# A gated graph network and three SAGE passes in one kernel: loads of the gated weights, the seam of first and second SAGE pass, and tiles cleared earlier

## The chip, the cores and the metric

The kernel runs on one core of one Trainium2 chip. A core has five engines that run their own instruction streams and wait for each other by semaphores: TensorE (PE, with its weight loads shown apart as PEld), VectorE (DVE), ScalarE (ACT), GpSimd (POOL) and SyncE (SP, which only issues DMAs here). ACT and POOL issue DMAs too. All DMAs run on the same 16 DMA engines. The metric is device time in microseconds, lower is better.

## What is computed

The input is a batch of 16 graphs with 1024 nodes and 128 features, and a dense adjacency of zeros and ones. Two layers follow each other, each with a residual and a layer norm:

```python
x = _layernorm(x + gnn0(x, adj, nodemask, ...))
x = _layernorm(x + gnn1(x, adj, nodemask, ...))

# gnn0: 4 gated layers
h = x
for i in range(4):
    hw = einsum('bnc,cd->bnd', h, weight[i])
    m = einsum('bjn,bjd->bnd', adj, hw)
    h = gru_cell(m, h, w_ih[i], w_hh[i], b_ih[i], b_hh[i])

# gnn1: a pattern of removed neighbours, and 3 SAGE passes on what is left
adj_d = adj * keep(adj > 0, mask)          # sequential over the rows
h1 = bn(relu(sage(x, adj_d, Wr1, Wx1, b1)))
h2 = bn(relu(sage(h1, adj_d, Wr2, Wx2, b2)))
h3 = bn(relu(sage(h2, adj_d, Wr3, Wx3, b3)))
out = concat([h1, h2, h3]) @ Wl + bl
# sage: ((adj_d @ x) / deg) @ Wr + x @ Wx + b, each row divided by its length
# bn: statistics over all graphs and nodes, so a pass ends before the next begins
```

The kernel is built on properties of the adjacency (zeros and ones, a pattern that settles at once). It tests them while it runs and has a general version for inputs where they don't hold. The tests are the "look" operations named below.

## The kernel before

**Stages.** A gated stage (class `Gated`, with the removal pattern, class `FixPoint`, woven into it), then the first, second and third SAGE pass (class `Sage`), and a last stage with the layer norm. Inside the gated stage and inside each pass the order of every engine's instructions is the one written in the code; each engine works through its list and waits in order. What stands between two passes (`Sage.run`, `weights`) is ordered by the tile scheduler.

**Lead-in of the gated stage.** `Gated.run` (from L1130) loads x of the first graph on POOL, calls `load_weights`, takes the first step of the removal pattern (four loads `f_a` on POOL), and loads the eight adjacency blocks `h_a` of the first graph on POOL. `load_weights` (L947) issues, for each of four layers, the weight (64 KB, `h_w`), `w_ih` and `w_hh` (192 KB each, in rows of 512 bytes), and then two small biases, all from ACT's queue. `prepare` transposes them on PE, multiplies the weight into `w_ih`, and copies the results by DVE (`w_ih`, `h_wi`) and ACT (`w_hh`, `h_wh`). Then PE begins the first layer's aggregation (L1092). ACT splits x into a rounded part and a rest (`begin_rows`, L1056) before its copies; POOL makes the rest (L1057) and only then loads the second graph.

**Gated layers.** Two graphs run in turn. A layer aggregates on PE (L1092), then computes the gates by products L1104, with sigmoids and tanh on ACT (L1113, L1119, L1122), two operations on DVE (L1116, L1118) and the state update on POOL (L1123 to L1125). All products use six PSUM banks `h_g`, in turn. While one graph's gates are computed, the other's state is transposed (L1037), rounded on ACT (L1025), and its rest is made on DVE (L1030). Steps of the removal pattern stand between these on DVE and ACT (L864, L866, L777, L737). Once a layer of the first graph ends, `load_test` loads one test block into `h_test` (a single buffer) on SP, and `check` tests it on DVE (L2028) within the second graph's next layer.

**First pass.** `slot(b, t)` writes 16 slots for each graph b, preparing graph b+1 in the same slots. It holds four buffers `p_a` for test blocks; `load_a` loads one on SP (L1491) and `check` tests it on DVE (L2028). For graph b the blocks 2 and 3 are loaded in slots 10 and 13 of the graph before, blocks 4 to 7 in slots 0, 2, 5 and 8, and the tests of blocks 2 to 7 are in slots 2, 5, 8, 10, 12 and 14. The chain of a graph: aggregation of x (slots 0, 1, 3, 4), copies to `s_ag` (slots 2 and 5, `evict`, L1601, two buffers in turn, shared with the copies of slot 15 that SP stores in slot 1 of the next graph, L1733), degrees, products `p_oa` and `p_ob` (slots 5 and 7), scaling on DVE (`scale_rows`, L1395 and L1396, slots 6 and 8), squares on ACT, rows (slots 7 and 9), their split (slots 8 and 10), the turn of the rows on PE with copy and statistics (`turn_r`, L1450, L1631, L1632, slots 11 and 13), and the second aggregation, of the rows (slots 9, 10, 12 and 14). SP stores the turned rows in slots 13 and 15 (L1717).

The order on SP within a slot is: `load_a` at its beginning, and the stores at its end.

**Seam.** After the last slot `Sage.run` computes the batch norm from the statistics and scales three weight matrices by it (`weights`, L1328 to L1366), with a small product `s_v` in a PSUM pool that takes over the first pass's banks, splits the result into three parts on DVE (L1343 to L1350), creates buffers, and clears the three `s_rho` tiles on POOL (L2014). Then `second` issues its loads (`load_second`, `load_bytes`) and its first products L1800, L1803, L1806.

Of the kernel before, what the change touches and what calls it, by code (L numbers as in the profile page):

```python
# [8 lines left out]
F32 = mybir.dt.float32  # L9
BF = mybir.dt.bfloat16  # L10
# [11 lines left out]
P = 128  # L22
B = 16
N = 1024
C = 128
NB = N // P
HF = 512
# [890 lines left out]
class Gated:  # L918
# [28 lines left out]
    def load_weights(self):  # L947

        nc, wk = self.nc, self.wk
        weight, w_ih, w_hh, b_ih, b_hh = self.given  # L950
        self.w = wk.tile([P, 4, P], F32, name="h_w")
        self.w_in = {}
        names = iter(n for n in "h_ms h_r h_z h_zh".split() for _ in range(2))
        for l in range(L0):
            nc.scalar.dma_start(self.w[:, l, :], weight[l])
            for n, src in enumerate((w_ih, w_hh)):
                t = wk.tile([C, HF], F32, name=next(names))
                t = self.w_in[l, n] = t[:, :3 * C].rearrange("p (g c) -> p g c", g=3)
                nc.scalar.dma_start(t, src[l].rearrange("(g p) c -> p g c", p=C))
        t = wk.tile([P, NB, C], F32, name="h_x", bufs=3)  # L960
        self.b_in = [t[:L0 * 3, i, :] for i in range(2)]
        for t, src in zip(self.b_in, (b_ih, b_hh)):
            nc.scalar.dma_start(t, src.rearrange("l (g c) -> (l g) c", c=C))

    def prepare(self):
        nc, ident = self.nc, self.cst["ident"]
# [24 lines left out]
    def load_test(self, n):  # L991
        if n < B * 2:
            self.test = self.wk.tile([P, N], F32, name="h_test", bufs=1)
            self.nc.sync.dma_start(self.test, self.adj[n // 2, n % 2 * P:(n % 2 + 1) * P, :])

    def check(self, n):
        junk = self.wk.tile([P, N], BF, name="h_junk", bufs=1)
# [212 lines left out]
class Sage:  # L1210
# [61 lines left out]
    def constants(self):  # L1272

        nc, ident, K = self.nc, self.cst["ident"], 3 * B
        const = self.const
        self.one16 = const([P, 1], 0.0, "s_one16", F16)
        nc.vector.memset(self.one16[:1, :], 1.0)
        nc.gpsimd.memset(self.row, 0.0)

        self.sel01 = const([10, 3, 6], 0.0, "s_sel01")  # L1280
        for i in range(3):
            nc.vector.tensor_copy(self.sel01[:, i, 3:], ident[:10, 3 * i:3 * i + 1].to_broadcast([10, 3]))
        self.ones = const([P, P], 0.0, "s_ones", BF)
        nc.vector.memset(self.ones[:6, :], 1.0)
        nc.gpsimd.memset(self.r6, 0.0)
        nc.gpsimd.memset(self.graph, 0.0)
        nc.vector.tensor_add(self.part6, ident[:6, 0:3], ident[:6, 3:6])
        self.part48 = const([K, 3], 1.0, "s_part48")
        for base, m in ((0, 1), (B - 1, -1)):
            nc.gpsimd.affine_select(self.part48, self.part48, pattern=[[-m * B, 3]], compare_op=ALU.is_ge,  # L1290
                                    fill=0.0, base=base, channel_multiplier=m)
        nc.vector.tensor_add(self.graph[:K, :], ident[:K, :B], ident[:K, B:2 * B])
        nc.vector.tensor_add(self.graph[:K, :], self.graph[:K, :], ident[:K, 2 * B:K])

        mask, junk = self.cst["mask"], self.wxp[:, 0, :].rearrange("p (a b) -> p a b", a=NB)
        nc.vector.scalar_tensor_tensor(junk, mask, 0.0, mask, op0=ALU.is_gt, op1=ALU.not_equal,
                                       accum_out=self.bad[:, BAD - 1:BAD])

        drop = self.wr2
        nc.vector.tensor_copy(drop, ident)  # L1300
        nc.vector.memset(drop[:1, :], -1.0)
        nc.vector.memset(drop[:1, :1], 0.0)
        nc.gpsimd.memset(self.mask48, 0.0)
        nc.vector.memset(self.mask48[:B, :], 1.0)
# [33 lines left out]
    def parts(self, v, part, out):  # L1338

        nc, shape = self.nc, list(v.shape)  # L1340
        rest = self.small.tile(shape, F32, name="s_rest")
        p = [self.small.tile(shape, BF, name=f"s_part{i}") for i in range(3)]
        nc.vector.tensor_copy(p[0], v)  # L1343
        nc.vector.tensor_sub(rest, v, p[0])
        nc.vector.tensor_copy(p[1], rest)
        nc.vector.tensor_sub(rest, rest, p[1])
        nc.vector.tensor_copy(p[2], rest)
        nc.vector.tensor_scalar(out, p[0], part[:, 0:1], None, op0=ALU.mult)
        for i in (1, 2):
            nc.vector.scalar_tensor_tensor(out, p[i], part[:, i:i + 1], out, op0=ALU.mult, op1=ALU.add)  # L1350

    def weights(self, l, v):

# [100 lines left out]
    def first(self):  # L1454

        nc, tc, cst = self.nc, self.tc, self.cst
        with ExitStack() as c:
            pool = lambda name, **k: c.enter_context(tc.tile_pool(name=name, **k))

            self.atp = [pool("p_at0", bufs=1)]  # L1460
            self.sp = pool("p_s", bufs=2)
            xp = pool("p_x", bufs=1)
            self.wk = pool("p_wk", bufs=2)
            self.atp.append(pool("p_at1", bufs=1))
            self.nrp = [pool(f"p_nr{i}", bufs=1) for i in range(2)]
            self.ap = pool("p_a", bufs=4)
            self.ps1 = pool("p_ps1", bufs=1, space=PSUM)
            self.ps2 = pool("p_ps2", bufs=2, space=PSUM)

            self.ps3 = pool("p_ps3", bufs=3, space=PSUM)  # L1470
            c.enter_context(tc.manual_schedule(engines={ET.PE, ET.DVE, ET.Activation, ET.Pool, ET.SP}))
            self.g = {}
            self.load_nr(0, 0)
            self.load_nr(0, 1)
            self.load_s(0)
            self.eps = self.const([P, 1], 1e-5, "s_eps")

            self.xh = xp.tile([P, NB, C], FR, name="p_xh")
            self.xl = xp.tile([P, NB, C], FR, name="p_xl")
            for t, v in ((self.xh, 1.0), (self.xl, 0.0)):  # L1480
                nc.vector.memset(t[:, :, :1].bitcast(F32), v)
            self.row = xp.tile([P, N], F16, name="p_row")
            self.constants()
            for b in range(-1, B):
                for t in range(16):
                    self.slot(b, t)
# [147 lines left out]
    def slot(self, b, t):  # L1634

        nc, g, n = self.nc, self.g.get(b), b + 1
        now, nxt = b >= 0, n < B

        if nxt:
# [3 lines left out]
                self.load_s(n + 1)  # L1643
            if t in (10, 13):
                self.load_a(n, 2 + t // 13)
        if now and t in (0, 2, 5, 8):
            self.load_a(b, (0, 2, 5, 8).index(t) + 4)

        if now:
            if t in (2, 5):  # L1650
# [11 lines left out]
        if now:  # L1662
# [3 lines left out]
            if t in (0, 1, 3, 4):  # L1666
                f, lo = t // 3, t in (1, 4)
# [5 lines left out]
            if t in (6, 8):  # L1673
                f = t // 8
# [6 lines left out]
            if t in (7, 9):  # L1681
                f = t // 9
# [2 lines left out]
                self.split_r(b, t // 10)  # L1685
            if t in (6, 8):
                g["ss", t // 8] = self.squares(g["o", t // 8])
            if t in (11, 13):
                self.turn_r(0, b, t // 13, self.ps1)
            if t in (9, 10, 12, 14):  # L1690
                part = g["rl"] if t in (10, 14) else g["rh"]
                js = range(4 * (t // 12), 4 * (t // 12) + 4)
# [5 lines left out]
        if nxt:  # L1698
# [5 lines left out]
                self.turn_x(n, t // 8)  # L1704
            if t in (7, 12):
                self.split_x(n, t // 12)
        if now and t in (2, 5, 8, 10, 12, 14):
            self.check(b, (2, 5, 8, 10, 12, 14).index(t) + 2)

        if now:  # L1710
            if t == 2:
                nc.sync.dma_start(self.at8[b, 1], g["b", 1])
            if t == 7:
                for i in range(3):
                    nc.sync.dma_start(self.rho[b, i:i + 1, :], g["rho"])
            if t in (13, 15):
                nc.sync.dma_start(self.rt[b, t // 15], g["rt", t // 15])  # L1717
        if nxt:
            if t == 10:
                nc.sync.dma_start(self.at8[n, 0], self.g[n]["b", 0])  # L1720
# [282 lines left out]
    def run(self):  # L2003
        tc, nc = self.tc, self.nc
        self.first()
        with tc.tile_pool(name="s_psw", bufs=1, space=PSUM) as ps:
            self.weights(1, ps.tile([6, C], F32, name="s_v6"))
        accp = self.ctx.enter_context(tc.tile_pool(name="s_acc", bufs=1))
        self.acc = accp.tile([P, B, NB, C], F32, name="s_acc")
        self.rt_kept = accp.tile([C, HF], F32, name="s_rtl")  # L2010
        self.ahead = self.ctx.enter_context(tc.tile_pool(name="s_ahead", bufs=1))
        self.rhos, self.layers = [self.ahead.tile([P, N], BF, name=f"s_rho{i}") for i in range(3)], 0
        for t in self.rhos:
            nc.gpsimd.memset(t, 0.0)  # L2014
        self.second()
        with tc.tile_pool(name="s_psw", bufs=1, space=PSUM) as ps:
            self.weights(2, ps.tile([6, C], F32, name="s_v6"))
        self.r3 = self.ctx.enter_context(tc.tile_pool(name="s_r3p", bufs=1)).tile([C, B, 2, HF], F32, name="s_r3")
        self.third()
        with tc.tile_pool(name="s_psw", bufs=1, space=PSUM) as ps:  # L2020
            r48 = self.head_weights(ps)
        self.last(r48)
# [94 lines left out]
```

## Time and profile before

| | us |
|---|---|
| median of 3 runs (2174.55 to 2177.75) | 2175.93 |
| the profiled execution | 2176.16 |
| its span, first to last instruction | 2174.3 |
| gated stage's first aggregation on PE begins at | 33.81 |
| first pass's last turn of rows copied at | 1742.93 |
| second pass's first product L1800 begins at | 1751.40 |

Times within the profile are microseconds from the start of the span. In a line of the timeline the columns are: start, duration, engine, line, operation, output<-inputs, shapes and count; in brackets stands how long the engine was idle before it and what it waited for. A line of the table of windows gives for a stretch: its length, then busy time and number of instructions of PE, PEld, DVE, ACT and POOL, the TensorE clock granted (1.00 is full), the busy share of the DMA engines, and GB/s.

### The profile page before, as it was taken

What the parts mean: (1) busy time and instruction counts of PE and PEld (TensorE: products, weight loads), DVE (VectorE), ACT (ScalarE), POOL (GpSimd) and SP (SyncE); (2) the same over time, 40 slices, a digit from 0 to 9 for tenths busy, and PEclk for the clock granted to TensorE, in tenths of its full rate; (3) what the DMA queues carried; (4) which work ended last, traced back from release to release, by engine and by line L of the source; (5) the groups of instructions that cost most, each with busy time, mean ns of one, the idle gap of its engine ahead of it and who ended that gap; (6) DMA issues with size and microseconds to landing.
All of it is one profiled execution on the core that took longest, in us unless ns stands there. A gap on an engine that the chain in (4) does not pass through costs nothing. (4 is left out here: it accounts for less than half of the span.)

```text
span 2174.3 us, 33161 instructions
## 1 busy us (share of the span) xinstructions
PE 2063.3 (95%) x10217; PEld 1438.1 (66%) x10217; DVE 1831.1 (84%) x4313; ACT 1312.8 (60%) x3142; POOL 1324.3 (61%) x1346
## 2 busy tenths in 40 slices
PE   6999999999999999999999978999999889999987
PEld 3666556666556665566655656777777768887876
DVE  4898998988998889998889978888888777676888
ACT  3657557566565656656566466666666545555757
POOL 4458558567467476476575456777777545555852
PEclk9999999999999999999999989999999999999989
DMA  8348356347446276455394349888888677775515
GB/s 258 77 93 252 92 126 225 82 133 214 101 143 195 75 210 155 96 190 132 79 266 104 74 166 318 305 297 307 304 305 306 209 243 271 265 262 185 158 40 157
DMA packets 233856, 406.16 MB, mean 187 GB/s; under 512 B 79042, under 2 KB 100196, under 8 KB 233668
## 3 DMA queue, kind: packets, MB, share of 16 engines
q1 hardware_dynamic: 187844, 284.37, 40.7%
q0 software_dynamic: 41472, 117.46, 20.1%
q10 hardware_dynamic: 4352, 2.11, 0.4%
q8 instruction: 83, 1.36, 0.3%
q14 instruction: 105, 0.86, 0.1%
HBM read 313.48 MB, written 109.25 MB: 194 GB/s over the span
## 5 line engine op out<-in xcount | busy, mean ns | idle before, releaser
L1104 PE MATMUL h_g<-h_h,h_wh 128*128 128x512 f32 x768 | 396.1, 597 | 3.3 <-DVE h_r L1116 3.3
L1104 PE MATMUL h_g<-h_ms,h_wi 128*128 128x512 f32 x768 | 392.3, 592 | 0.0
L1123 POOL TENSOR_TENSOR h_zh<-h_r,h_h 128x512 f32<-128x512 f32 x126 | 174.1, 1382 | 257.9 <-ACT h_r L1119 254.7
L737 DVE TENSOR_TENSOR_SCAN f_rank<-f_a,f_first,f_pd 128x1024 f16<-128x1024 bf16 x128 | 299.4, 2345 | 4.2
L1092 PE MATMUL h_g<-h_a,h_hi 128*128 128x512 f32 x1024 | 278.6, 413 | 1.1 <-DMA h_a<-in_adj_dram 1.0
L1536 POOL CAST p_b<-p_at 128x512 uint8<-128x512 f32 x256 | 219.4, 878 | 84.3 <-DVE p_at L1528 52.3
L1104 PEld LDWEIGHTS h_g<-h_ms,h_wi 128*128 128x128 f32 x768 | 145.6, 190 | 184.2 <-issue 168.6
L1092 PE MATMUL h_g<-h_a,h_lo 128*128 128x512 f32 x1024 | 261.9, 393 | 0.4 <-DVE h_lo L1030 0.4
L1092 PEld LDWEIGHTS h_g<-h_a,h_hi 128*128 128x128 f32 x1024 | 190.1, 188 | 61.7 <-issue 21.0
L1092 PEld LDWEIGHTS h_g<-h_a,h_lo 128*128 128x128 f32 x1024 | 189.8, 188 | 39.0 <-DVE h_lo L1030 0.8
L1104 PEld LDWEIGHTS h_g<-h_h,h_wh 128*128 128x128 f32 x768 | 133.4, 190 | 100.3 <-issue 72.9
L1125 POOL TENSOR_TENSOR h_h<-h_h,h_zh 128x512 f32<-128x512 f32 x126 | 179.9, 1427 | 9.9
L1119 ACT ACTIVATE h_r<-h_r,h_bi 128x512 f32<-128x512 f32 x128 | 92.4, 722 | 150.1 <-DVE h_r L1118 150.1
L1124 POOL TENSOR_TENSOR h_zh<-h_z,h_zh 128x512 f32<-128x512 f32 x126 | 162.0, 1285 | 9.9
L1095 ACT COPY h_ms<-h_g 128x512 f32<-128x512 f32 x128 | 73.8, 576 | 150.7 <-PE h_g L1092 150.7
L1403 ACT ACTIVATE s_junk<-s_o 128x128 bf16<-128x128 f32 x256 | 76.1, 298 | 141.6 <-DVE s_o L1396 141.6
L910 ACT ACTIVATE f_u<-f_rank,f_q 128x128 f16<-128x128 f16 (+7 forms) x128 | 110.6, 867 | 69.7 <-DVE f_rank L850 69.7
L2028 DVE SCALAR_TENSOR_TENSOR p_junk<-p_a 128x1024 bf16<-128x1024 f32 x96 | 125.8, 1311 | 0.0
L1803 PE MATMUL q_ob<-s_wxp,q_xt 128*128 128x256 f32 x512 | 123.5, 385 | 0.0
L778 POOL TENSOR_SCALAR_AFFINE_SELECT f_both<-f_both 128x512 bf16<-128x512 bf16 x32 | 20.4, 639 | 164.2 <-DVE f_both L777 164.2
L1528 DVE SCALAR_TENSOR_TENSOR p_at<-p_nr,p_u 128x128 fp32r<-128x128 bf16 (+1 forms) x192 | 102.4, 543 | 20.2 <-ACT p_at L1520 14.8
L887 ACT ACTIVATE f_pd<-f_rank,f_q 128x128 f32<-128x128 f16 x128 | 59.1, 462 | 96.6 <-DVE f_q L701 93.4
(273 smaller groups left out, 4900.9 us busy)
## 6 DMA issues: line engine op xcount, KB each, us to landing
h_a<-in_adj_dram POOLq DMA_DIRECT2D x128, 512.0 KB, 9.1
p_a<-in_adj_dram SPq DMA_DIRECT2D x96, 512.0 KB
f_a<-in_adj_dram POOLq DMA_DIRECT2D x128, 256.0 KB, 6.5
e_nr<-f_nr SPq DMA_DIRECT2D x128, 256.0 KB
p_nr<-e_nr SPq DMA_DIRECT2D x32, 1024.0 KB
h_test<-in_adj_dram SPq DMA_DIRECT2D x32, 512.0 KB
s_at<-p_b SPq DMA_DIRECT2D x32, 512.0 KB
s_ag<-s_ag SPq DMA_DIRECT2D x64, 256.0 KB
```

The costliest lines, as they stand in the source:

```text
L737: nc.vector.tensor_tensor_scan(out, a, other[:, 0, 0:1].to_broadcast([P, N]), start, op0=ALU.add, op1=ALU.bypass)
L910: nc.scalar.activation(u[:, :n1], rank[:, g, :n1], AF.Abs, bias=q[:, 1, g:g + 1], scale=q[:, 0, g:g + 1])
L1092: nc.tensor.matmul(pm[f], part[:, j, :], st.adj[j][:, half[f]], start=(j == 0 and n == 0), stop=(j == NB - 1 and n == 1))
L1104: nc.tensor.matmul(pg, lhs, rhs, start=(i == 0), stop=(i == len(mm) - 1))
L1119: nc.scalar.activation(r, r, AF.Tanh, bias=bias(self.bi, 2))
L1123: aid.tensor_tensor(d, r, h, ALU.subtract)
L1124: aid.tensor_tensor(d, z, d, ALU.mult)
L1125: aid.tensor_tensor(h, h, d, ALU.add)
L1528: self.nc.vector.scalar_tensor_tensor(g["at"][:, j, c0:c0 + low], v[:, j, c0:c0 + low], 0.0, pu[:, :low], op0=ALU.is_lt, op1=ALU.is_lt)
L1536: self.nc.gpsimd.tensor_copy(g["b", f][:, j, :], g["at"][:, j, f * HF:(f + 1) * HF].bitcast(F32))
L1803: nc.tensor.matmul(pb[:, i], g["xt"][:, f, blk], self.wxp, start=(i % 2 == 0), stop=False)
L2028: nc.vector.scalar_tensor_tensor(junk, a, 0.0, a, op0=ALU.is_gt, op1=ALU.not_equal, accum_out=bad[:, c:c + 1])
```

## The change

There are six edits.

1. The loads of `w_hh` and of the biases are issued by SP instead of ACT.
2. The first test block of the gated stage is loaded by POOL instead of SP; the others stay on SP.
3. The three `s_rho` tiles move into the pool that lives through all passes, and are cleared with the other constants at the beginning of the first pass, behind the clearing of `row`, instead of between the passes.
4. For the last graph of the first pass, test blocks 4 to 7 are loaded in slots 0, 0, 1 and 2 and the tests are made in slots 0 to 5; the turns of the rows are in slots 10 and 12 and their stores in slots 11 and 13.
5. The small product of the first seam gets the fourth bank of its pool, where it had the first.
6. `idle` issues products into a bank that nobody reads, four ahead of `weights(1)` and six behind it.

```diff
@@ load_weights
-                nc.scalar.dma_start(t, src[l].rearrange("(g p) c -> p g c", p=C))
+                (nc.scalar, nc.sync)[n].dma_start(t, src[l].rearrange("(g p) c -> p g c", p=C))
...
-            nc.scalar.dma_start(t, src.rearrange("l (g c) -> (l g) c", c=C))
+            nc.sync.dma_start(t, src.rearrange("l (g c) -> (l g) c", c=C))
@@ load_test
-            self.nc.sync.dma_start(self.test, self.adj[n // 2, n % 2 * P:(n % 2 + 1) * P, :])
+            (self.nc.sync if n else self.nc.gpsimd).dma_start(self.test, self.adj[n // 2, n % 2 * P:(n % 2 + 1) * P, :])
@@ constants
         nc.gpsimd.memset(self.row, 0.0)
+        for t in self.rhos:
+            nc.gpsimd.memset(t, 0.0)
@@ new function
+    def idle(self, junk, n):
+
+        for i in range(n):
+            self.nc.tensor.matmul(junk, self.cst["ident_b"], self.mask48[:, :HF], start=True, stop=True)
@@ first
             self.row = xp.tile([P, N], F16, name="p_row")
+            self.rhos, self.layers = [self.one.tile([P, N], BF, name=f"s_rho{i}") for i in range(3)], 0
@@ slot
-        if now and t in (0, 2, 5, 8):
-            self.load_a(b, (0, 2, 5, 8).index(t) + 4)
+        tail = b == B - 1
+        slots = (0, 0, 1, 2) if tail else (0, 2, 5, 8)
+        if now and t in slots:
+            for k in range(4):
+                if slots[k] == t:
+                    self.load_a(b, k + 4)
...
-            if t in (11, 13):
-                self.turn_r(0, b, t // 13, self.ps1)
+            slots = (10, 12) if tail else (11, 13)
+            if t in slots:
+                self.turn_r(0, b, slots.index(t), self.ps1)
...
-        if now and t in (2, 5, 8, 10, 12, 14):
-            self.check(b, (2, 5, 8, 10, 12, 14).index(t) + 2)
+        slots = (0, 1, 2, 3, 4, 5) if tail else (2, 5, 8, 10, 12, 14)
+        if now and t in slots:
+            self.check(b, slots.index(t) + 2)
...
-            if t in (13, 15):
-                nc.sync.dma_start(self.rt[b, t // 15], g["rt", t // 15])
+            slots = (11, 13) if tail else (13, 15)
+            if t in slots:
+                nc.sync.dma_start(self.rt[b, slots.index(t)], g["rt", slots.index(t)])
@@ run
-            self.weights(1, ps.tile([6, C], F32, name="s_v6"))
+            junk = [ps.tile([P, HF], F32, name=f"s_junk{i}") for i in range(3)][2]
+            v = ps.tile([6, C], F32, name="s_v6")
+            self.idle(junk, 4)
+            self.weights(1, v)
+            self.idle(junk, 6)
...
-        self.rhos, self.layers = [self.ahead.tile([P, N], BF, name=f"s_rho{i}") for i in range(3)], 0
-        for t in self.rhos:
-            nc.gpsimd.memset(t, 0.0)
```

## The prediction

> **What bounds the kernel now.** I read four views. The page first: TensorE (PE) is busy 95% of the span. The chain of waits holds one piece at the very end, so the chain is built from the timeline. The table of windows then shows where PE's share counts: in the gated stage (33 to 1275 us) PE is busy 297 of every 300 us, so a microsecond before that stage moves everything behind it, and so does a stall within it.
>
> ```profile
> span 2174.3 us, 33161 instructions
> PE 2063.3 (95%) x10217; PEld 1438.1 (66%) x10217; DVE 1831.1 (84%) x4313; ACT 1312.8 (60%) x3142; POOL 1324.3 (61%) x1346
> ...
> 33.00:333.00 300.00, 297.31 (x1121) 182.86 (x1122) 266.91 (x560) 180.54 (x329) 173.99 (x168) 1.00 0.50 132
> ```
>
> The timeline of 0 to 60 us shows the lead-in. See that ScalarE (ACT) is held by issuing fourteen small loads until 23.5 us, that PE waits for the weights, and that DMA is saturated (share over 1, about 385 GB/s) until 27 us.
>
> ```profile
> 18.00:21.00 3.00, 0.79 (x4) 0.39 (x2) 0.29 (x1) 0.00 (x0) 0.00 (x0) 1.00 1.13 384
> ...
> 13.23 0.90 PE L974 MATMUL h_g<-ident,h_r 128*128 128x128 f32 x3 [5.40 <-DMA h_r<-in_L_gnn_w_ih_dram]
> 17.68 0.90 PE L974 MATMUL h_g<-ident,h_r 128*128 128x128 f32 x3 [3.55 <-DMA h_r<-in_L_gnn_w_hh_dram]
> 23.50 1.28 ACT L1056 ACT_TABLE_LOAD   x1 [23.50 <-DMA h_z<-in_L_gnn_w_ih_dram]
> 23.55 0.87 PE L974 MATMUL h_g<-ident,h_z 128*128 128x128 f32 x3 [4.76 <-DMA h_z<-in_L_gnn_w_ih_dram]
> 33.81 2.09 PE L1092 MATMUL h_g<-h_a,h_hi 128*128 128x512 f32 x8
> 57.49 1.30 POOL L1125 TENSOR_TENSOR h_h<-h_h,h_zh 128x512 f32<-128x512 f32 x1
> 57.83 2.04 DVE L2028 SCALAR_TENSOR_TENSOR h_junk<-h_test 128x1024 bf16<-128x1024 f32 x1
> 67.89 0.68 DVE L1030 TENSOR_TENSOR h_lo<-h_g,h_hi 128x512 fp32r<-128x512 f32 x1
> ```
>
> The timeline of 1719 to 1757 us shows the seam. See what the first copy of the last graph waits for, who works beside the weights' product, and the clock.
>
> ```profile
> 1720.15 1.24 SPq L1733 DMA_DIRECT2D s_ag<-s_ag  x2
> 1725.10 0.59 ACT L1601 COPY s_ag<-p_ag 128x512 f32<-128x512 f32 x1 [4.06 <-DMA s_ag<-s_ag]
> 1730.76 0.67 DVE L1395 TENSOR_TENSOR s_o<-p_oa,s_rdeg 128x512 f32<-128x512 f32 x1
> 1746.05 2.87 POOL L2014 MEMSET s_rho<- 128x1024 bf16 x3 [4.12 <-DMA s_rt<-s_rt]
> 1747.14 0.83 DVE L1336 TENSOR_SCALAR s_wr<-s_wr,s_ab 128x128 f32<-128x128 f32 x1
> 1751.43 0.98 PE L1800 MATMUL q_oa<-s_wr,q_agi 128*128 128x128 f32 x3 [0.73 <-PE s_v L1366]
> 1756.12 0.69 DVE L1396 TENSOR_TENSOR s_o<-q_ob,s_o 128x512 f32<-128x512 f32 x1 [1.85 <-PE q_ob L1806]
> ...
> 1748.00:1749.00 1.00, 0.00 (x0) 0.00 (x0) 1.00 (x5) 0.00 (x0) 0.92 (x1) 0.50 1.04 397
> ```
>
> **What the Trainium skill says.** "DMA: Bandwidth & Descriptors", section on queues, rings and completion order: each DMA engine "round-robins between the queue rows it has work for", packet by packet. The trace agrees: from 17.7 to 23.5 us the ACT queue landed 256 KB (44 GB/s) of 385 GB/s, 11%, which is one 512-byte row for each 4096-byte row of the POOL queue. "SBUF — State Buffer", two separate sides: VectorE (DVE) in a two-port mode and GpSimd (POOL) lock a shared port pair for a whole instruction. The trace agrees: the 128x128 scaling at 1747.14 took 0.83 us beside POOL's memsets, the same form at 2104.13 0.28 us. "TensorE: Matmul & The Clock Gate", what's actually happening: an idle window of about 3.4 us halves the clock. Here PE stopped at 1744.75 and the window from 1748 shows 0.50, full again near 1754.7.
>
> **The change part by part**, against the profiled execution (2176.16 us, span 2174.3; the median shown is 2175.93, 0.2 less).
>
> *Gated weights' queue.* Six of ACT's fourteen loads go to SP, a third queue beside POOL's, so the weights take two turns in three instead of one in two. Before, the ACT queue moved 56 rows per DMA engine by about 6.3 us, then one per 0.184 us (56 rows from 13.2 to 23.5). After, the last weight is ACT's eighth load, row 128. I take 50 rows by 6.3; 46 at 0.22 us beside SP's 96 (0.184 plus 0.035 to 0.045 for the extra row, below the 0.055 per row seen once the adjacency tapers off): 16.4; the last 32 at 0.184: 22.3 us. ACT, with eight issues, is free long before and does the splits of x early. From the last weights' transposes (28.02) to the first aggregation (33.81) are 5.8 us of PE and copies, unchanged. New start 28.2: **-5.6 us**. Bounds: DMA now ends at 27.8; 512 KB less (the test load leaves) is 1.3 us at 400 GB/s, so the adjacency is in near 27.5 and its last block is used 1.7 us after the start: at most -8.0. If the weights only gain the room of the test load: -1.3. The second stream's loads start earlier too; they had 8 us of slack (landed by 45, used at 52.6).
>
> *First test's load on POOL.* It was on SP at 1.24 us. On POOL it stands behind the state update that ends at 58.8. Nobody waits behind it on POOL (next work 66.6), but DVE's test, at 57.8, does. A 256 KB load on a quiet POOL queue took at least 4.0 us to land; with 256 KB more at 400 GB/s, 4.6. The test then runs 63.4 to 64.6 and DVE continues 4.8 us late. Behind it: four pairs L864/L866 (1.1 each), L777 (0.5), L1116, L1118 and L1030 (0.85, 0.7, 0.7), which ends at 71.7 instead of 68.57 (before, the pairs had 1.35 of waits that vanish). The six banks go round: the product at 68.82 takes the bank that L1030 reads, so PE stalls 2.9 us, for good. Bounds: landing in 3.0 (the least of any POOL transfer of x) costs 1.3; 7.9 costs 6.2. I take **+2.9**.
>
> *Tiles cleared in lead-in.* Three memsets of 0.95 us now stand on POOL behind that of the row (1278.15). POOL was idle 1.83 of these 2.85 us; its memset of the mask ends 1.3 us later, and DVE, which had 0.16 to 0.8 us of waits there, starts its unit (1284.46) 0.5 us late: **+0.5** (0 to 1.5). POOL's next cast waited 5.8 us for a store anyway.
>
> *Last tests and loads moved.* On SP, load 6 of the last graph now stands ahead of the two stores of s_ag, and it waits for test 2, which DVE can begin at 1722.2 and end near 1723.5. The first store so leaves at 1724.0 instead of 1720.15, behind one load more on a saturated queue. Its data (by the sum of the windows' GB/s) move by 1727.1; before they were due at 23.6 and the release came 1.5 later, so the copy at 1725.10 goes to 1728.6: +3.5 (2.5 to 4.4). Below nothing it can't go: the store is only put later. On DVE four tests of 1.14 us now stand between the copy and L1395, in place of one: L1395 comes 6.3 us after the copy instead of 5.66: 1734.9, +4.1. PE idles from 1726.2 to 1729.9, 3.7 us; I take it that the clock drops as at 1748, half speed for 3.3 us, of which 0.7 reach L1395. Before, the four later tests delayed the rows by only 0.1.
>
> *Turns moved, own bank, memset gone, junk matmuls.* Measured from L1395. The last turn comes before the third part of the aggregation, so the statistics are complete 12.0 us after L1395 (14.5 before). The six scalings take about 1.3 instead of 1.9 us. PE finishes at +14.6 (14.0), and with a product near +16 doesn't go cold. The ten junk matmuls (0.22 each) fill an idle PE; if the scheduler puts them earlier, up to 1 us. What is late next is a transfer: the loads of the second pass wait for the release of the first's tiles (+14.2), and land as before 4.0 (s_ag) and 5.5 us (s_rt) after issue; so L1803 at +19.7, L1806 ends at +22.0, L1396 at +22.1 instead of 25.4: -3.3 (-2.3 to -4.3). Seam: 4.1 + 0.7 - 3.3 = **+1.5**.
>
> Sum: -5.6 + 2.9 + 0.5 + 1.5 = -0.7 us, so 2175.2.
>
> **Rivals.** (1) *The seam gives what it saves.* If the release of the s_ag buffer isn't the brake (store still in time), L1395 is 0.6 late and the seam is -2.7: sum -4.9, 2171.0. For it: PE's own result was ready at 1724.4, only 0.7 before the copy. Against: the wait of 4.06 us ended by that store. (2) *The weights come no sooner*, because DMA is saturated anyway: -1.3 instead of -5.6: +3.6, 2179.5. For: the share over 1. Against: the 11%. (3) *The test load ends on the other side*: one mechanism, DVE's in-order wait at 57.8, priced at 1 us per us of landing beyond 1.7. From a landing of 5.3 us the whole is slower than before; if it lands in 11.3, as POOL's adjacency loads did at the start, it costs 9.6 and the sum is +6.0, 2181.9. For: POOL's loads are often that long. Against: DMA moves 0 to 5 GB/s from 48 to 60 us. (4) *DVE's slack takes the test's wait*: +0.4: -3.2, 2172.7. For: DVE is busy 16.8 of 20 us there. Against: PE's slack on L1030 is 0.25 us.
>
> **How the numbers follow.** Forecast 46% (its own range 2172 to 2178), rival 1 22%, rival 2 14%, rival 3 9%, rival 4 9%. About 0.2%, 4.4 us, is what a measurement of this kernel can tell from no change. Faster by more: two thirds of rival 1, a third of 4, a twelfth of the forecast, and their mixtures: 24%. Slower by more: 0.4 of rival 2, most of 3, a twelfth of the forecast, and a rest: 19%. Within: 57%. The range 2170.0 to 2180.5 takes in the rivals' times save the upper part of 3.
>
> **What would show it.** L1092's first start near 28 us; the first L2028 waiting for h_test until 60 to 64 and a PE wait of some us near 65 (after the shift); in the seam (shifted) the copy L1601's wait for s_ag of 7 us instead of 4, L1395 some 4 us later against the last stage's begin, no POOL memset, PE clock 1.00 at the product. Wrong would make it: L1092 at 32 or later; the copy not waiting; or release of the second pass's loads ruled by something else.

## The result, and the profile after it

The changed kernel takes 2182.35 us (median of 8 runs, 2180.25 to 2184.56) against 2175.68 us before (8 runs on the same chip, 2173.92 to 2179.19): ratio 1.0030, 95% interval 1.0021 to 1.0038. It is 6.7 us slower, outside the range given. The profiled execution took 2182.17 us, its span is 2180.4 us, 6.1 more than before. From the profile page of the changed kernel (busy time of each engine, its share of the span, instructions):

```profile
PE 2063.6 (95%) x10226; PEld 1438.0 (66%) x10227; DVE 1833.3 (84%) x4313; ACT 1312.9 (60%) x3142; POOL 1325.4 (61%) x1347
```

TensorE (PE) is as busy as before to 0.3 us; what came is idle time. To find it I set the two timelines beside each other and took the start of the same product in both. In this table and below, the lead-in is the stretch from the gated stage's last transposes to the first aggregation of the first pass, and a product is called cold when it takes up to twice its usual time at a granted clock of 0.50:

| stretch, from product to product | before, us | after, us | difference |
|---|---|---|---|
| span start to first L1092 | 33.81 | 27.59 | -6.2 |
| to the first L1037 past 70 us (first test lies between) | 47.45 | 48.18 | +0.7 |
| to L1037 of the gated stage's end | 1193.19 | 1192.91 | -0.3 |
| **lead-in: to the first aggregation of the first pass** | 23.21 | 35.95 | **+12.7** |
| first pass, to the low part of its last graph | 424.74 | 422.12 | -2.6 |
| **seam: to the first L1806 (after: L1821)** | 33.30 | 37.30 | **+4.0** |
| second and third pass, to the last stage | 351.15 | 349.49 | -1.7 |
| last stage | 67.5 | 66.9 | -0.6 |

The start came near the predicted time: the last weights are turned at 20.35 instead of 28.02 us, and the first aggregation begins at 27.59. The timeline of the kernel before, then of the changed one:

```profile
28.02 1.49 PE L974 MATMUL h_g<-ident,h_zh 128*128 128x128 f32 x6
...
29.51 3.46 PE L981 MATMUL h_g<-h_wi,h_w 128*128 128x384 f32 x8
```

```profile
20.35 1.51 PE L974 MATMUL h_g<-ident,h_zh 128*128 128x128 f32 x6 [4.70 <-DMA h_zh<-in_L_gnn_w_ih_dram]
...
21.88 4.87 PE L981 MATMUL h_g<-h_wi,h_w 128*128 128x384 f32 x8
...
27.59 2.09 PE L1092 MATMUL h_g<-h_a,h_hi 128*128 128x512 f32 x8
```

Next, the first test: one line of the kernel before, then the changed kernel (L2044 there is L2028 before):

```profile
68.82 1.02 PE L1104 MATMUL h_g<-h_h,h_wh 128*128 128x512 f32 x2
```

```profile
52.52 0.59 POOL L994 DMA_DIRECT2D h_test<-in_adj_dram  x1
...
56.23 1.23 DVE L2044 SCALAR_TENSOR_TENSOR h_junk<-h_test 128x1024 bf16<-128x1024 f32 x1 [4.54 <-DMA h_test<-in_adj_dram]
...
62.41 0.74 DVE L1116 SCALAR_TENSOR_TENSOR h_r<-h_g,h_bh,h_r 128x512 f32<-128x512 f32 x1
...
63.21 1.12 PE L1104 MATMUL h_g<-h_h,h_wh 128*128 128x512 f32 x2 [0.45 <-DVE h_r L1116]
...
63.87 0.68 DVE L1030 TENSOR_TENSOR h_lo<-h_g,h_hi 128x512 fp32r<-128x512 f32 x1
```

The load is issued behind the state update and lands 3.7 us later, and DVE waits 4.54 us for it. But PE waits only 0.45 us, and its product is 0.6 us later than its old place shifted by the start (68.82 - 6.22 = 62.60).

Now the lead-in, where nearly all was lost. The timeline of the kernel before, which was not shown yet:

```profile
1274.45 0.60 PE L1037 MATMUL h_g<-ident,h_h 128*128 128x128 f32 x4
...
1278.15 0.94 POOL L1278 MEMSET p_row<- 128x1024 f16 x1 [3.35 <-ACT h_z L1122]
1278.26 0.07 DVE L1481 MEMSET p_xh<- 128x8 f32 x1
...
1282.97 0.55 POOL L1072 DMA_DIRECT2D e_sum<-h_x  x1 [0.52 <-DVE h_x L1070]
...
1284.73 0.59 PE L1515 MATMUL p_u<-ident_b,p_nr 128*128 128x128 bf16 x4 [1.72 <-DVE p_at L1528]
...
1289.29 3.95 POOL L1536 CAST p_b<-p_at 128x512 uint8<-128x512 f32 x7 [5.76 <-DMA e_sum<-h_x]
```

POOL begins p_row as soon as ACT's L1122 is done, and DVE begins p_xh without a wait; only POOL's casts (L1536) wait for the store of e_sum, 5.76 us that nobody else feels. The same stretch after:

```profile
1268.68 0.60 PE L1037 MATMUL h_g<-ident,h_h 128*128 128x128 f32 x4
...
1277.63 0.54 POOL L1072 DMA_DIRECT2D e_sum<-h_x  x1 [8.59 <-DVE h_x L1070]
...
1285.30 0.95 POOL L1278 MEMSET p_row<- 128x1024 f16 x1 [7.13 <-DMA e_sum<-h_x]
1285.37 0.07 DVE L1488 MEMSET p_xh<- 128x8 f32 x1 [8.04 <-DMA e_sum<-h_x]
...
1286.19 2.78 POOL L1280 MEMSET s_rho<- 128x1024 bf16 x3
...
1289.20 0.17 DVE L1294 TENSOR_TENSOR s_graph<-ident 48x16 f32<-48x16 f32 x1 [2.64 <-POOL s_graph L1288]
...
1292.16 0.58 PE L1523 MATMUL p_u<-ident_b,p_nr 128*128 128x128 bf16 x4 [14.48 <-DVE p_at L1536]
```

Now the memsets of p_row and p_xh themselves wait for that store. It was issued at 1277.63 and took 7.5 us to land, while the first pass's matrices were loading (DMA share 0.98 from 1275 to 1285). The same store took 6.1 us in the kernel before, and 7.7 us in run 4 below, where PE feels nothing of it: what counts is who waits for it. DVE sits idle 8.04 us. Behind it come POOL's three memsets of s_rho, for which DVE waits 2.64 us more, and PE is idle 14.48 us. That the memset of a new tile waits for a transfer of the stage before points to where the tile lies.

Last the seam: three products of the kernel before, then the timeline of the changed kernel (L1595 is now L1603, L1601 L1609, L1395 L1402, L1396 L1403):

```profile
1722.40 1.98 PE L1595 MATMUL p_ag<-p_at,p_xl 128*128 128x512 f32 x8
...
1726.51 2.11 PE L1595 MATMUL p_ag<-p_at,p_xl 128*128 128x512 f32 x8
...
1735.94 2.08 PE L1595 MATMUL p_ag<-p_at,p_rh 128*128 128x512 f32 x8 [2.12 <-ACT p_rh L1444]
```

```profile
1723.71 4.68 SPq L1499 DMA_DIRECT2D p_a<-in_adj_dram  x3
...
1726.75 1.98 PE L1603 MATMUL p_ag<-p_at,p_xl 128*128 128x512 f32 x8
...
1728.48 0.86 SPq L1748 DMA_DIRECT2D s_ag<-s_ag  x2
...
1733.89 0.58 ACT L1609 COPY s_ag<-p_ag 128x512 f32<-128x512 f32 x1 [8.49 <-DMA s_ag<-s_ag]
...
1735.31 3.76 PE L1603 MATMUL p_ag<-p_at,p_xl 128*128 128x512 f32 x8
...
1741.21 0.67 DVE L1402 TENSOR_TENSOR s_o<-p_oa,s_rdeg 128x512 f32<-128x512 f32 x1
...
1746.40 3.69 PE L1603 MATMUL p_ag<-p_at,p_rh 128*128 128x512 f32 x8 [2.13 <-ACT p_rh L1451]
...
1757.30 0.38 PE L1371 MATMUL s_v<-s_wr,s_beta 128*6 128x128 f32 x2
...
1764.53 0.69 DVE L1403 TENSOR_TENSOR s_o<-q_ob,s_o 128x512 f32<-128x512 f32 x1 [1.86 <-PE q_ob L1821]
```

And a line of the table of windows (the granted clock of PE is the third number from the end):

```profile
1733.00:1735.00 2.00, 0.00 (x0) 0.00 (x0) 0.49 (x2) 1.08 (x2) 0.00 (x0) 0.50 1.01 409
```

SP is held by three loads until 1728.4, since they wait for tests on DVE that free their buffers. The first store of s_ag so leaves 1.7 us after the low part of the last graph has begun (1728.48, against 1726.75 for that product); before it left 2.3 us ahead of it (1720.15 against 1722.40). The copy waits 8.49 instead of 4.06 us, PE stands still from 1730.5 to 1735.2, and the clock falls to 0.50. The two cold products (3.76 and 3.69 us) took 2.11 and 2.08 us in the kernel before. At the weights' product the clock is 1.00 again, and the product takes 0.38 us instead of 0.58; the turns made earlier, the own bank, the idle products and the absent memsets stand together in this trace.

### The profile page after: what moved, and what is told of

It reads as the page before. It is cut to its first block, busy times and chain, and to the rows that moved or that the text cites. A ratio compares the mean times of both kernels' runs of the same rounds, so it can differ in the third digit from the quotient of the medians.

```text
span 2180.4 us, 33182 instructions
## 1 busy us (share of the span) xinstructions
PE 2063.6 (95%) x10226; PEld 1438.0 (66%) x10227; DVE 1833.3 (84%) x4313; ACT 1312.9 (60%) x3142; POOL 1325.4 (61%) x1347
## 5 line engine op out<-in xcount | busy, mean ns | idle before, releaser
L1092 PE MATMUL h_g<-h_a,h_hi 128*128 128x512 f32 x1024 | 278.4, 413 | 0.4 <-DMA h_a<-in_adj_dram 0.4
L1092 PE MATMUL h_g<-h_a,h_lo 128*128 128x512 f32 x1024 | 262.2, 393 | 0.1
L1092 PEld LDWEIGHTS h_g<-h_a,h_hi 128*128 128x128 f32 x1024 | 190.1, 188 | 60.8 <-issue 21.0
L1092 PEld LDWEIGHTS h_g<-h_a,h_lo 128*128 128x128 f32 x1024 | 189.6, 188 | 39.3 <-DVE h_lo L1030 1.3
L2044 DVE SCALAR_TENSOR_TENSOR p_junk<-p_a 128x1024 bf16<-128x1024 f32 x96 | 125.9, 1311 | 0.1
L1523 PE MATMUL p_u<-ident_b,p_nr 128*128 128x128 bf16 x1024 | 96.8, 223 | 21.0 <-DVE p_at L1536 18.7
```

The source lines that it names most:

```text
L1092: nc.tensor.matmul(pm[f], part[:, j, :], st.adj[j][:, half[f]], start=(j == 0 and n == 0), stop=(j == NB - 1 and n == 1))
L1523: nc.tensor.matmul(pu[:, i * P:(i + 1) * P], v[:, 4 * f + i, j * P:(j + 1) * P], self.cst["ident_b"], start=True, stop=True)
L2044: nc.vector.scalar_tensor_tensor(junk, a, 0.0, a, op0=ALU.is_gt, op1=ALU.not_equal, accum_out=bad[:, c:c + 1])
```

## Experiments

Twelve kernels in three groups, each timed beside the kernel before on one chip; a ratio is to the kernel before, with its 95% interval. "Stretch" numbers are those of the table above, from each run's own profiled execution, which is one execution among several.

The place of the tiles in the on-chip memory, bytes per partition, as the programs allot it:

| pool | before | with s_rho in s_one |
|---|---|---|
| p_s | 73,440 to 81,632 | 79,584 to 87,776 |
| p_x (p_xh, p_xl, p_row) | 81,632 to 91,872 | 87,776 to 98,016 |
| h_wk of the gated stage | 96,832 to 160,320 | the same |

The three tiles, 2,048 bytes each, came out of a pool that lies below the first pass's pools and pushed all of these up by 6,144 bytes. p_x now reaches 1,184 bytes into h_wk, and h_wk also holds h_x, the source of the e_sum store. My theory: it is this reach that costs, not the memsets. Rivals: the memsets; the shift as such; an end of the gated stage that comes early and meets the same store.

**1. The start alone.** Only the edits of L959, L963 and L994.

> The kernel before with the start of the gated stage alone: the hidden weights and the biases on SP's queue, the first test's load on POOL's. The traces put this part at -6.2 us at the first aggregation and +0.7 at the test (-5.5 after it), and no other stage is touched: about 2170.3 us. If what was gained at the start were lost again at the gated stage's end whatever is done to the tiles (an earlier end meets the same store), it would be 2175.7, and PE's idle time in the lead-in of the first pass would grow to some 14 us here too.

2169.51 us, 0.9971 (0.9958 to 0.9983), as expected. The lead-in was 23.38 us, PE did not wait there. An early end of the gated stage loses nothing: that rival is out, and the start's gain reaches the end of the program.

**2. The tiles alone**, allotted in s_one and cleared in the lead-in.

> The kernel before with the three s_rho tiles taken from s_one and cleared on POOL in the lead-in of the first pass, nothing else. My theory (the place of the tiles: the pool p_x is pushed into the region of the gated stage's h_wk and all lead-in work waits for its last store): the first pass begins some 11 us later, POOL's three memsets are gone from the seam (up to -1.5 there): 2185 us, 2183 to 2188. The prediction's own price (three memsets behind one another, place without effect): +0.5, 2176.

2187.20 us, 1.0048 (1.0031 to 1.0064), with a lead-in of 36.61 us. This part alone costs 10.9 us, the whole change 6.7.

**3 and 4. Place without memsets.** An unused tile ahead of the first pass's pools; nothing else.

```diff
+            pad = pool("p_pad", bufs=1).tile([P, 1536], F32, name="p_pad")
             self.atp = [pool("p_at0", bufs=1)]
```

> The kernel before with an unused tile of 6144 bytes per partition put ahead of the first pass's pools, so that p_x ends at 98,016 instead of 91,872 (h_wk begins at 96,832); no instruction is added or moved. Place alone: +8 to +10, as the change's +11.4 less some 2 us of memsets ahead of the DVE work: 2184.5 us, with POOL's memset of p_row and DVE's of p_xh waiting for the store of e_sum. If the memsets were the cause: 2175.7, no change.

> As the last, with 4096 bytes in place of 6144: p_x ends at 95,968, 864 bytes short of h_wk. If it is the reach into h_wk that counts: 2175.7, no change. If any shift of the first pass's tiles costs (other pools over other buffers, other banks): most of what the 6144 bytes cost.

With 6,144 bytes: 2183.52 us, 1.0031 (1.0018 to 1.0043). With 4,096 bytes: 2177.62 us, 1.0008 (0.9999 to 1.0017). The timeline of the first, then of the second:

```profile
1284.08 0.54 POOL L1072 DMA_DIRECT2D e_sum<-h_x  x1 [8.61 <-DVE h_x L1070]
...
1291.72 0.07 DVE L1482 MEMSET p_xh<- 128x8 f32 x1 [7.94 <-DMA e_sum<-h_x]
...
1291.83 0.95 POOL L1278 MEMSET p_row<- 128x1024 f16 x1 [7.21 <-DMA e_sum<-h_x]
...
1296.42 0.59 PE L1516 MATMUL p_u<-ident_b,p_nr 128*128 128x128 bf16 x4 [12.31 <-DVE p_at L1529]
```

```profile
1279.32 0.94 POOL L1278 MEMSET p_row<- 128x1024 f16 x1 [3.35 <-ACT h_z L1122]
1279.43 0.07 DVE L1482 MEMSET p_xh<- 128x8 f32 x1
...
1284.42 0.55 POOL L1072 DMA_DIRECT2D e_sum<-h_x  x1 [0.80 <-DVE h_x L1070]
...
1286.18 0.58 PE L1516 MATMUL p_u<-ident_b,p_nr 128*128 128x128 bf16 x4 [1.72 <-DVE p_at L1529]
```

No instruction differs between these two, and none from before; only their order on POOL and DVE does: with 6,144 bytes the memset of p_row stands behind the store's issue. With 6,144 bytes p_row and p_xh wait for e_sum and PE is idle 12.31 us, with 4,096 they don't and it is 1.72 us as before; the lead-ins are 33.78 and 23.42 us. So it is the reach, with a step between 4,096 and 6,144 bytes, and not the shift. Note p_xh: it lies from 87,776 to 91,872 and touches no tile of h_wk. In run 4 the same bytes belong to p_xh and p_xl, and neither waits; here p_xh waits all the same, so in these runs the release of the old region is taken by the pool and not by the tile. The difference of runs 2 and 3 (36.61 - 33.78) is what the three memsets cost once they stand behind that wait: 2.8 us. The times show less than the lead-in does: run 3 is 7.2 us (3.9 to 9.4) above the kernel before, its lead-in 10.6 us longer.

**5. The changed kernel with p_row moved.** One line: p_row's tile from a pool of its own behind p_a, so that p_x ends at 95,968.

```diff
-            self.row = xp.tile([P, N], F16, name="p_row")
+            self.row = pool("p_rowp", bufs=1).tile([P, N], F16, name="p_row")
```

> The changed kernel with one edit: p_row's tile comes from a pool of its own behind p_a, so that p_x ends at 95,968 again, short of h_wk; the three memsets stay where the change put them. If the reach into h_wk is the cause of the lead-in's loss: the lead-in gives back what the 6144 bytes cost (7 to 10), less what three memsets cost there: 2173 to 2175, against 2182.4 of the change. The prediction's own price for the memsets (+0.5) would give 2173; if the memsets cost the 2.6 us that DVE waited for them in the changed kernel, 2175. If the shift of all pools is the cause: 2182.

2173.00 us, 0.9990 (0.9983 to 0.9997): from slower than before to slightly faster, 9.4 us below the changed kernel. Its timeline:

```profile
1271.88 0.94 POOL L1278 MEMSET p_row<- 128x1024 f16 x1 [0.57 <-DVE f_junk L880]
...
1272.76 2.73 POOL L1280 MEMSET s_rho<- 128x1024 bf16 x3
...
1274.78 0.07 DVE L1488 MEMSET p_xh<- 128x8 f32 x1
...
1277.49 0.16 DVE L1294 TENSOR_TENSOR s_graph<-ident 48x16 f32<-48x16 f32 x1
...
1281.53 0.59 PE L1523 MATMUL p_u<-ident_b,p_nr 128*128 128x128 bf16 x4 [1.72 <-DVE p_at L1536]
```

POOL does all three memsets in a row (2.73 us) and nobody waits for them. The lead-in is 23.43 us against 23.21 before: they cost 0.2 us at most, which is within the scatter of the kernels that don't reach into h_wk (23.04 to 23.55).

**6 to 8. The seam in parts**: all its edits; the moved loads and tests alone; the turns, own bank and idle products alone. The s_rho tiles stay as before in all three.

> The kernel before with the seam's edits alone: last tests and loads moved, turns and their stores moved, own bank and ten idle products; the s_rho tiles stay where they were and are cleared at the seam. The trace of the change puts the seam at +4.0 us (first product of the second pass, less the offset of the last graph ahead of it): +4 and up to 1 more for the memsets that stay: 2179.5 to 2181. The prediction's sum for the seam: +1.5 plus that 1, 2178. If the whole of the change's loss came from the lead-in: 2176.

> Of the seam's edits only the last graph's loads and tests moved (slots 0 to 5). My reading of the trace: SP stands behind tests until 1728.5, the stores of s_ag leave 4 us later, the copy and the rows with it, and PE idles twice long enough to lose its clock: +6 to +7.5: 2182 to 2183.5. By the prediction's terms (+3.5, +0.6 of tests, +0.7 of clock): 2180.7. If the copy did not wait for that store: 2176.3.

> Of the seam's edits only the turns and their stores a slot earlier, the own bank of the weights' product and the ten idle products. The trace of the change puts this part at -3.5 (prediction -3.3) beside cleared tiles; here POOL's three memsets stay at the seam and lock the port of DVE's scalings, some 0.5 to 1 us of it back: 2172.5 to 2173.5. If the gain hangs on the memsets' absence: 2175.7.

All: 2178.38 us, 1.0007 (0.9998 to 1.0016). Loads and tests: 2181.37 us, 1.0027 (1.0019 to 1.0035). Turns and bank: 2175.38 us, 0.9997 (0.9988 to 1.0005). The three effects expected from the trace of the change were all larger than these; two figures worked out from the prediction's own terms, 2178 for all and 2180.7 for loads and tests, came close. The stretch of the seam was 35.91, 40.31 and 30.73 us. The copy in the run with loads and tests alone, and PE in the one with turns and bank:

```profile
1727.92 0.58 ACT L1601 COPY s_ag<-p_ag 128x512 f32<-128x512 f32 x1 [8.07 <-DMA s_ag<-s_ag]
```

```profile
1744.74 2.12 PE L1355 MATMUL s_junk<-s_mask,ident_b 128*128 128x512 bf16 x8
1748.64 0.38 PE L1369 MATMUL s_v<-s_wr,s_beta 128*6 128x128 f32 x2 [1.78 <-DVE s_beta L1381]
```

The first shows the wait for the store doubled by the loads' move alone. In the second the idle products stand before the weights' product and it runs warm (0.38 us), POOL's memsets still being at the seam. Its gain of 2.6 us in the trace is not shown by its times, whose interval holds 1; what shows it is run 6 against run 7, 3.0 us apart with intervals that don't touch.

**9. Loads behind the stores.** As run 7, with the slots of loads 6 and 7 behind the stores of s_ag.

```diff
-        slots = (0, 0, 1, 2) if tail else (0, 2, 5, 8)
+        slots = (0, 0, 2, 2) if tail else (0, 2, 5, 8)
```

> The loads and tests of the last graph moved as in the run that moved only these, but loads 6 and 7 behind the two stores of s_ag on SP (slots 0, 0, 2, 2 for 0, 0, 1, 2), so that no store stands behind a test. If SP's order is what cost 5 us (7 in its trace): the copy waits 4 us for the store as before, PE keeps its clock, and what stays is the tests on DVE, +0.6: 2177. If the tests ahead of the rows on DVE are the cost: 2180 or more.

2177.12 us, 1.0007 (1.0000 to 1.0014), against 1.0027 (1.0019 to 1.0035) in run 7. SP and the copy in its timeline:

```profile
1718.96 2.60 SPq L1491 DMA_DIRECT2D p_a<-in_adj_dram  x2
...
1721.65 0.86 SPq L1738 DMA_DIRECT2D s_ag<-s_ag  x2
...
1726.26 0.59 ACT L1601 COPY s_ag<-p_ag 128x512 f32<-128x512 f32 x1 [5.61 <-DMA s_ag<-s_ag]
```

The first store leaves at 1721.65, 0.35 us ahead of the low part's product at 1722.00; two loads are still before it. Before it was 2.3 us ahead, in the changed kernel 1.7 behind. The copy comes 4.6 to 5.4 us after that store is issued in these three kernels (before 1720.15 to 1725.10, here 1721.65 to 1726.26, changed 1728.48 to 1733.89), and 4.4 to 5.8 us in all nine in which the store ends its wait. So the store's place on SP sets the copy, once the store is late: in the other five kernels it stands at its old place, and the copy waits for PE's product instead (3.41 us). The wait of 5.61 us is longer than the 4 expected, since two loads are still ahead of the store. The tests ahead of the rows on DVE are all here still, and 1.5 us (0 to 3) is what is left of the loss.

**10 to 12. The start without the test's load on POOL, and two sums of what seemed worth keeping.** Run 11 is start plus turns and own bank; run 12 adds the s_rho tiles with p_row in its own pool, cleared last on POOL.

> The hidden weights and biases on SP's queue, with the first test's load left on SP at 1.24 us. The stall of 0.7 at the test goes; the load's 512 KB now move before the start, on the third queue's share: 1.3 us at 400 GB/s if DMA is what bounds, nothing if the weights' turns are. Weights bound: 2168.8, start at 27.6. DMA bound: start at 28.9, 2170.

> The start of the gated stage (measured alone at -6.8) and the turns with the own bank together, without the moved loads and tests and without the tiles in the lead-in. The two lie 1700 us apart and should add: -9.5, 2166.7. If what is gained at the start is lost at the seam, 2169.5.

> What the runs so far say is worth keeping: weights' queue and first test on POOL (-6.8), turns and own bank (-2.5 in its trace), and the s_rho tiles in s_one with p_row in its own pool, cleared last of POOL's lead-in behind the last store of e_sum, where POOL waits anyhow. The memsets leave the seam: up to -1 more there. 2166 to 2167, against 2167.2 without the tiles; 2169 if clearing costs in the lead-in even there.

Run 10: 2170.90 us, 0.9981 (0.9972 to 0.9990); the stretch with the first test is 47.45 us, as before, so the 0.7 us go with the load's old place. The first aggregation begins at 28.39 us, between the two expected starts, and the time is nearer that of the later one; what bounds the weights is not settled. Its times don't tell it from run 1. Run 11: **2167.24 us, 0.9955 (0.9938 to 0.9971)**, the fastest, over 4 runs only. Run 12: 2170.18 us, 0.9977 (0.9968 to 0.9986). Both beat both kernels. Run 12 misses the expected 2166 to 2167. That clearing earlier brings anything on top is not shown: the two spans are 2168.2 and 2168.1 us, the seam's stretch is 32.51 us with the tiles cleared earlier and 31.73 without, and the intervals meet.

## Why the prediction was wrong, point by point

*Start, -5.6: right, in part by luck.* First L1092 at 27.59 (predicted 28.2). Over the profiled executions it came at 26.30 to 29.77 in the six kernels with the edit and at 33.52 to 35.02 in the eight without; the means are 28.4 and 34.2, -5.8 us. Rival 2 (weights no sooner) is out. But in the changed kernel's trace two terms missed and made up for each other: the last weights were there 2 us sooner (20.35 against 22.3), and from there to the first aggregation it took 7.2 us and not the "5.8, unchanged". These 1.4 us more lie in the eight products L981 (4.87 instead of 3.46); why they are slower is open. (One bound there is also off by 1 us: 27.8 less 1.3 is 26.5, not 27.5. Nothing rests on it.)

*First test's load, +2.9: right wait, size off.* It was 0.7 to 1.0 us in the five kernels that have it. The load landed in 3.7 us where 4.6 was taken, and that is 0.9 of the difference. The rest is the last term, "the product at 68.82 takes the bank that L1030 reads, so PE stalls 2.9 us". The trace shows that product released by L1116, which ends 1.4 us before L1030 does; DVE was 2.2 us late at both.

*Tiles cleared in lead-in, +0.5 (0 to 1.5): this step failed.* The prediction priced "three memsets of 0.95 us" on POOL and for these it was right: 0.2 us in run 5. It did not ask where the tiles lie, and so put the move of the other pools at nothing. Taken from a pool below the first pass's, the tiles moved p_x into h_wk, whose last user is a store in flight, and the lead-in became 12.7 us longer: 10.6 of it the wait (33.78 - 23.21 in run 3) and the rest the memsets queued behind it. Runs 3, 4 and 5 show this. It alone carries the prediction out of its range: with it mended, the change measures 2173.0, inside 2170.0 to 2180.5. That is 2.7 us (0.7 to 3.7) below the kernel before, where the forecast was 0.7; the first test's overpriced stall is of about that size.

*Last tests and loads, +3.5 at the copy, +4.1 at L1395, +0.7 of clock: right, short in the changed kernel's trace.* On the scale of the last graph's products the copy came 4.4 us later (the bound given), L1395 6.1. Between these two, 1.66 us were added; the one cold product explains 1.65, and nothing is left for the four tests. So the term too small in the trace was the clock, 1.65 us instead of 0.7, and this product was cold in all four kernels with late stores (3.52 to 3.76 us in the changed kernel and runs 5, 6 and 7). The second cold product, another 1.6 us, does not go with the edits: runs 5 and 6 have the same ones there, and it took 2.11 and 2.13 us. The times agree with the prediction: run 7 lost 5.1 us (4.1 to 7.6) where the terms give about 4.8. "TensorE: Matmul & The Clock Gate" of the Trainium skill, what's actually happening, has the clock halved by an idle window of about 3.4 us; the trace agrees for the first drop (PE idle 4.6 us), but the second came after 2.13 us of idle time (see the last section).

*Turns, bank, memsets gone, -3.3: near in the trace, not shown alone.* From L1395 to L1396 it took 23.3 us instead of 25.4, with the second cold product's 1.6 us in it, so the edits gave some 3.6 us if all of that product reached the end. By the times, the turns and the bank gained 3.0 us behind moved loads (run 6 against 7), and nothing that can be told from zero without them (run 8).

Sum of the stretches: -6.2 + 0.7 - 0.3 + 12.7 - 2.6 + 4.0 - 1.7 - 0.6 = +6.0, the span's +6.1 within rounding. The -2.6 of the first pass belongs to no edit of that stretch: it took 422.1 to 425.6 us over all the kernels. The three with a long lead-in lie at 422.1, 422.2 and 423.3, so some of the loss may come back there; by the times, the mend of run 5 is worth 9.4 us, by the lead-in 12.5. The -1.7 is a product at L1803 that was cold before (3.54 us) and warm after (1.89). No rival of the prediction was what happened. The third gave 2181.9, near the result, by a late landing that did not occur.

What stays open: why the seam takes between 32.9 and 36.0 us in five kernels that leave it alone (33.30, 32.93, 33.14, 35.97, 35.90). The two long ones have a shifted tile layout, a copy that waits 0.7 us longer for the store, and cold products. The layout alone doesn't cause the longer wait: in run 2 the first pass's tiles lie where they do in run 3, and its copy waits 3.41 us, for PE. Why the store landed later in runs 3 and 4 is not known.

## What to carry to other kernels

A tile has a price beyond its instructions: ask which pool it comes from, what that pool pushes, and whose region the pushed ones reach into. If a stage's first instructions begin to wait for a transfer of the stage before, look there first, and try one unused tile of the same size to see it. When loads are moved ahead on a queue, each that waits for a buffer holds the stores behind it; put the stores whose buffers someone waits for in front.

## What the runs showed of the hardware

The same idle gap of PE is sometimes free and sometimes costs 1.5 us. Runs 8 and 11 have the same code at the seam. Before the first product of the last graph's rows PE is idle for the same time. The timeline of run 11, then of run 8:

```profile
1730.84 3.58 PE L1600 MATMUL p_ag<-p_at,p_rh 128*128 128x512 f32 x8 [2.12 <-ACT p_rh L1449]
```

```profile
1735.66 2.12 PE L1600 MATMUL p_ag<-p_at,p_rh 128*128 128x512 f32 x8 [2.13 <-ACT p_rh L1449]
```

After 2.12 us of idle time the product takes 3.58 us in run 11 (granted clock 0.50 from 1732 to 1734); after 2.13 us it takes 2.12 us in run 8 (1.00 from 1734 to 1738). All fourteen kernels have this gap, 2.12 to 2.20 us in their profiled executions; the product behind it took 2.08 to 2.13 us in seven of them and 2.53 to 3.69 us in the other seven. So an idle time below the 3.4 us of the page named above can cost, and whether it does is not in the code. That page has the window run freely, so where the stretch falls in it would explain this; no run here tests it. It makes a seam like this one scatter by 1 to 2 us from execution to execution, so one trace doesn't settle an edit of that size.

Second, the store of e_sum (512 KB) takes 3.4 us from issue to landing in the median of the sixteen. The last of them took 7.5 us in the changed kernel and 6.1 us in the kernel before, beside the first pass's loads (DMA share 0.98 in the changed kernel). A region whose release hangs on such a store comes free that much later.
